# Channel stage: three images as one stationary operand on the way back, and the row sums of the two parities as products on their own rows of the array

## The chip, the core and the metric

The kernel runs on one NeuronCore of a Trainium2 chip. A core has a tensor engine (PE in the profile; PEld is its loading of stationary operands, which overlaps), a vector engine (DVE), a scalar engine (ACT), GpSimd (POOL), and queues that issue transfers (SP's above all). SBUF and PSUM have 128 partitions; PE reads SBUF and writes PSUM, which the kernel uses as eight banks of 512 fp32 numbers a partition. The metric is the device time of one execution in microseconds; all numbers here are fp32.

A product on PE has a stationary operand (K rows by M columns, loaded into the array) and a moving one (K rows by N columns). The result has M partitions and N numbers each. An fp32 product shows as two passes in the profile, each with its own load. Beside the whole array (128 by 128) a product may use half of its rows (64 by 128: K up to 64, at partition 0 or 64) or half of its columns (128 by 64: M up to 64).

## The reference

The input x has 32 images of 192 channels of 56 by 56 pixels. Four layers are applied, each as x = x + f(groupnorm(x)), with 32 groups of 6 channels: agent attention, a bidirectional linear recurrence (RWKV), a shift by whole pixels with a 3 by 3 Gaussian for every four channels, and a long convolution. The channel stage of the kernel computes the last two:

```python
# layer 2: every channel is shifted by the rounded offset and blurred with a 3x3 kernel of the rest
x = x + _L2_conv_ref(_gn(x), L2_conv_offset)
# layer 3: a 55x55 kernel k, made by a small network from positions, applied per channel over FFTs
xf = jnp.fft.rfft2(x, s); kf = jnp.fft.rfft2(k[0], s)
y = jnp.fft.irfft2(xf * kf[None], s)
x = x + y[..., Kh // 2:Kh // 2 + H, Kw // 2:Kw // 2 + W] + bias * _gn(x)
```

## The kernel before

The kernel first makes the spectra of the long filters (make_filter), then runs attention, then the recurrence (scan_pairs), which writes x to DRAM channel by channel, and then the channel stage (channel_blocks), which holds the 32 images of one channel at a time.

A channel's tile x has 114 partitions: 57 for the even images (56 pixel rows and one row of the group means) and 57 for the odd ones, the two "parities" s. Along a partition stand 16 pairs of images, 56 pixels each. The steps, with their lines:

- shift: the blur and shift are two products per quad of images (two pairs): L1589 with the quad as stationary operand and the row matrix moving, L1596 (DVE) scales into `turned`, L1607 with `turned` as stationary operand and the column matrix moving, L1615 adds to x, L1616 takes sums.
- centre: L1633 (DVE) subtracts the mean into `padded`, whose pixel rows are 64 apart, L1635 (ACT) squares, L1636 sums the squares. L1624 (PE) brings sums of the six channels of a group together, for the mean and for the variance.
- analyse: the row sums (`_rows_to_spectra`, L1757): a quad of `padded` is the stationary operand, 114 rows by 128 columns, and the cosines and sines `f1` move, 168 columns: 42 frequencies, cosine and sine, for each parity, with zeros for the other parity's rows. Three quads fill a PSUM tile; L1763 (ACT) copies it to `y` in four pieces. Then L1655 makes `re` and `im` in three batches of 5, 5 and 6 pairs, and six operations on DVE for each batch (L1662 to L1668) multiply with the filter's spectrum into `real` and `imag`, 84 partitions by 32 images of 42 numbers.
- synthesise, the way back: L1681 takes a pair of images (84 columns) of `real` or `imag` as stationary operand, 32 products a channel, four pairs to a PSUM tile, which L1688 (ACT) copies to `z`, 84 partitions (2 images of 42). L1698 multiplies `z` (moving, eight pairs, 448 columns) with `f4` (stationary, 84 rows by 114 columns), so that the even image of a pair goes to partitions 0 to 56 and the odd one to 57 to 113; L1700 and L1701 (DVE) scale and add to x, and two transfers write the channel out.

The loop at the end of channel_blocks interleaves these: channels come in groups of six, and while group n is shifted (two channels in each of three slots) and centred (two in each of three slots), group n - 1 is analysed, a channel a slot, and the channel of the slot before is synthesised. The four generators are advanced in a fixed pattern of steps; the order in which the instructions finally stand in each engine's queue is set when the program is built, by the Tile framework's scheduler, which also assigns the PSUM banks. At run time each engine takes its queue in order. PSUM has four banks for the tiles named ps (shift, row sums, L1624, the way back), two for re and two for im.

make_filter uses the same `_rows_to_spectra` six times near the start, with two PSUM buffers.

## Time and profile before

| what | value |
|---|---|
| median of 3 runs | 12293.82 us (12292.39 to 12298.46) |
| the profiled execution | 12294.66 us, span of its instructions 12292.8 us |
| mean granted TensorE clock | 0.966 of full speed |
| busy, of the span | PE 92%, PEld 58%, DVE 88%, ACT 50%, POOL 18% |
| channel stage, from its first instruction to the end | 8372 to 12292.8 us |
| of it, 10000 to 11000 us | PE 988.2, PEld 764.3, DVE 866.4, ACT 355.4, POOL 83.7 us busy; clock 1.00 |
| DMA in the stage | 17% of its engines, 43 GB/s |

Times are from the start of the span. "busy" of PE is the union of its passes, whose ends are modelled; how far apart passes start says more. A group is shown as line, engine, operation, output<-inputs, shape (rows*columns of the stationary operand, then what moves), count, busy time, mean length and the idle time of the engine just before it with what ended that. In an order of time, a line gives start, length, engine and the merged instructions.

### The profile page before, as it was taken

Reading aid. Unit: us, or ns where it says so; the run is one execution under the profiler, and the core shown is the slowest. Engines: PE = TensorE matmul, PEld = TensorE weight load, DVE = VectorE, ACT = ScalarE, POOL = GpSimd, SP = SyncE. Lnnn points to the kernel's source line nnn. Section 1 sums busy time; section 2 is a strip of 40 time slices with the busy share of each in tenths; the row PEclk is TensorE's granted clock in tenths of the full one; section 3 lists DMA queues with packets and bytes.
Section 4 is the critical chain, followed back from the end, with each engine's and each line's share of the span. In section 5 each row is a group of like instructions: output and inputs, shape, how many; then the busy total and the mean of one; then the engine's idle time right before and its main releaser. Section 6 shows DMA issues by size and latency. Waiting matters only on the chain. (4 is left out here: it accounts for less than half of the span.)

```text
span 12292.8 us, 164375 instructions
## 1 busy us (share of the span) xinstructions
PE 11329.2 (92%) x62734; PEld 7107.7 (58%) x62734; DVE 10836.4 (88%) x15489; ACT 6205.0 (50%) x11808; POOL 2250.7 (18%) x2228
## 2 busy tenths in 40 slices
PE   7999999999999999788888888888999999999999
PEld 3555555655555555333333333336777777777777
DVE  6888888888888887999999999997888888888888
ACT  3555555555555554566666666663333333333333
POOL 0000000000000000655555555551000000000000
PEclk9999999999999999999999999999999999999999
DMA  2111111111111111244344433442111111111111
GB/s 69 40 42 46 52 41 40 40 40 40 40 40 40 42 50 44 75 103 100 95 97 103 101 94 97 103 101 65 44 41 45 41 44 42 44 42 44 42 43 29
DMA packets 930055, 719.69 MB, mean 59 GB/s; under 512 B 770325, under 2 KB 807236, under 8 KB 920124
## 3 DMA queue, kind: packets, MB, share of 16 engines
q1 hardware_dynamic: 919020, 683.39, 21.7%
q10 hardware_dynamic: 10240, 25.70, 0.8%
q8 instruction: 500, 8.19, 0.3%
q14 instruction: 295, 2.42, 0.1%
HBM read 403.47 MB, written 240.65 MB: 52 GB/s over the span
## 5 line engine op out<-in xcount | busy, mean ns | idle before, releaser
L572 DVE SCALAR_TENSOR_TENSOR o<-v_a,att_w,o 128x896 f32<-128x896 f32 (+1 forms) x1024 | 1053.8, 1029 | 418.6 <-ACT v_a L546 291.5
L1763 ACT COPY y<-ps 64x252 f32<-64x252 f32 (+1 forms) x2376 | 808.2, 340 | 1135.0 <-PE ps L1757 1104.8
L1681 PE MATMUL ps<-fixed,real 84*84 84x112 f32 x6144 | 1090.9, 259 | 0.0
L1681 PE MATMUL ps<-fixed,imag 84*84 84x112 f32 x6144 | 1089.5, 259 | 0.0
L1688 ACT COPY z<-ps 84x448 f32<-84x448 f32 x768 | 405.6, 528 | 1218.5 <-PE ps L1681 1217.0
L1086 POOL MEMSET f<- 128x1 f32 x96 | 8.9, 99 | 4726.3 <-DMA st_c<-st 4721.3
L1681 PEld LDWEIGHTS ps<-fixed,real 84*84 84x84 f32 x6144 | 784.0, 153 | 134.2 <-issue 95.8
L1681 PEld LDWEIGHTS ps<-fixed,imag 84*84 84x84 f32 x6144 | 763.8, 153 | 0.0
L1079 ACT ACTIVATE q<-q 128x784 f32<-128x784 f32 x384 | 328.2, 855 | 802.5 <-DVE q L1074 633.1
L834 PE MATMUL ps<-sq,fixed 128*128 128x392 f32 x512 | 297.3, 743 | 428.6 <-ACT sq L1157 428.6
L572 DVE SCALAR_TENSOR_TENSOR o<-v_c,att_w,o 128x448 f32<-128x448 f32 (+1 forms) x1024 | 635.0, 620 | 5.1
L585 PE MATMUL ps<-xs_a,gk_a 128*98 128x448 f32 (+1 forms) x1536 | 637.1, 495 | 0.0
L589 ACT ACTIVATE pr<-ps,low 98x896 f32<-98x896 f32 (+1 forms) x384 | 352.3, 918 | 559.9 <-DVE low L587 559.9
L586 PE MATMUL ps<-xs_c,gk_c 125*98 125x448 f32 (+1 forms) x1536 | 631.6, 492 | 0.0
L1547 POOL TENSOR_TENSOR mat<-tap,tap 114x114 f32<-114x114 f32 x96 | 40.8, 425 | 3166.1 <-PE ps L1607 2313.2
L677 PE MATMUL ps<-gq_a,xs_a 128*112 128x294 f32 x1792 | 602.8, 417 | 19.2 <-DVE pq L682 19.2
L1698 PE MATMUL ps<-z,fixed 84*114 84x448 f32 x1536 | 608.8, 539 | 0.0
L834 PE MATMUL ps<-x,weights 128*128 128x392 f32 x1536 | 577.4, 519 | 27.5 <-DVE bv L1108 14.2
L678 PE MATMUL ps<-gq_c,xs_c 125*112 125x294 f32 x1792 | 594.5, 412 | 0.0
L1655 PE MATMUL re<-y,fixed 128*84 128x420 f32 (+1 forms) x1152 | 532.3, 543 | 8.7 <-ACT y L1763 7.6
L1655 PE MATMUL im<-y,fixed 128*84 128x420 f32 (+1 forms) x1152 | 526.9, 538 | 0.0
L690 ACT ACTIVATE pq<-pq 112x1176 f32<-112x1176 f32 x224 | 265.3, 1184 | 498.9 <-DVE pq L682 376.0
(367 smaller groups left out, 29245.2 us busy)
## 6 DMA issues: line engine op xcount, KB each, us to landing
x<-x SPq DMA_DIRECT2D x576, 392.0 KB
x<-x SPq DMA_DIRECT2D x512, 196.0 KB
x<-x SPq DMA_DIRECT2D x192, 399.0 KB
out_x<-x SPq DMA_DIRECT2D x384, 196.0 KB
x<-in_x SPq DMA_DIRECT2D x32, 1568.0 KB
x<-x SPq DMA_DIRECT2D x32, 1568.0 KB
x<-in_x SPq DMA_DIRECT2D x64, 392.0 KB
rd<-rd ACTq DMA_DIRECT2D x128, 196.0 KB
```

The source lines that it names most:

```text
L572: nc.vector.scalar_tensor_tensor(dst, tap(i), dww[:, t, i : i + 1], dst, ALU.mult, ALU.add)
L585: mm(ps[P2, h, :n], g[:, cols], xs_a[j][:, px], start=True, stop=False)
L586: mm(ps[P2, h, :n], gk_c[0:KC, 2 * j + h, cols], xs_c[j][0:KC, px], start=False, stop=True)
L589: nc.scalar.activation(pr[:, :, :n], ps[P2, :, :n], AF.Exp, bias=low[:, j, p : p + 1], accum_out=sums[:, j, p : p + 1])
L677: mm(ps[:SUB, i, :HA], xs_a[j][:, px], g, start=True, stop=False)
L678: mm(ps[:SUB, i, :HA], xs_c[j][0:KC, px], gq_c[0:KC, 2 * j + (q + i) // ns], start=False, stop=True)
L834: mm(out, aa, srcs[t][h], start=True, stop=False)
L1655: nc.tensor.matmul(ps[:, : n * 84], f2[:, i, :], y[:, i0 : i0 + n].rearrange("p g s u -> p (g s u)"), start=True, stop=True)
L1681: nc.tensor.matmul(ps[:84, i * 2 * S : (i + 1) * 2 * S], part[:, i0 + i].rearrange("p s u -> p (s u)"), f3[:, m, :], start=(m == 0), stop= ...
L1688: nc.scalar.copy(z[:, i0 : i0 + n].rearrange("p g m w -> p (g m w)"), ps[:84, : n * 2 * S])
L1698: nc.tensor.matmul(got, f4[:, m, :], z[:, i0 : i0 + n, m, :], start=(m == 0), stop=(m == 1))
L1763: nc.scalar.copy(y[64 * m : 64 * m + 64, 2 * g0 + i : 2 * (g0 + n) : 2], got[64 * i : 64 * i + 64, :, :, m, :])
```

## The change

Even and odd images now stand at partitions 0 to 56 and 64 to 120 of x, `padded` and the constants (PR, the number of partitions in use, goes from 114 to 121), with zeros between.

- Row sums: each quad gives two products instead of one, rows 0 to 56 and rows 64 to 120, each on its half of the array's rows, with only 84 columns moving. Four quads make a batch, with one PSUM tile for each parity, and each tile is copied to `y` in four pieces of 168 elements: 16 copies a channel in place of 12.
- Way back: the stationary operand of L1681 is three images (126 columns) instead of two, so 11 in place of 16 (the last one has two images), and `z` has 126 partitions.
- Last product: three images to a column of `z` no longer match even and odd. For nine (then seven) pairs of images there is a product for the pairs whose images 0 and 1 stand in one column, one for the pairs with images 1 and 2, and for the pairs that lie across two columns two products on half of the array's columns each. `f4` holds a stationary operand for each.
- Shift: the stationary operand of L1607 has 121 columns; `turned` is 64 apart; the x tiles are fifteen fixed ones, cleared once (partitions 32 to 63), as are the two `turned` tiles, and a channel is loaded by two transfers.

```diff
-    (114, (2 * 2 * NF,)), (128, (2, 2 * NF)), (84, (2, 2 * S)), (84, (2, 114)), (114, (114,)), (114, (114,)),
...
+PR = 64 + S + 1
...
+    (PR, (2 * NF,)), (128, (2, 2 * NF)), (84, (2, 2 * S)), (126, (2, 2 * PR + 128)), (PR, (PR,)), (PR, (PR,)),
...
-    f4 = np.zeros((2, NF, 2, 2, R))
-    for s in range(2):
-        f4[s, :, 0, s, :S], f4[s, :, 1, s, :S] = weight * cos, -weight * sin
+    f4 = np.zeros((3, NF, 2, 2 * PR + 128))
+    for i, c in ((0, 0), (1, 64), (1, PR), (2, PR + 64), (2, 2 * PR), (0, 2 * PR + 64)):
+        f4[i, :, 0, c : c + S], f4[i, :, 1, c : c + S] = weight * cos, -weight * sin
...
+    shifted = [cp.tile([PR, NI, S], F32, name=f"x{i}", tag=f"x{i}") for i in range(15)]
+    for t in shifted:
+        nc.vector.memset(t[32:64], 0.0)
+    sides = [cp.tile([2 * S, NG, 2, 64], F32, name=f"turned{i}", tag=f"turned{i}") for i in range(2)]
+    for t in sides:
+        nc.vector.memset(t[:, :, :, S + 1 : 64], 0.0)
+
...
 
         c = q.n * GROUP + j
         rows, cols = matrices(c // 4)
-        x = xp.tile([PR, NI, S], F32, name="x", tag="x")
-        nc.sync.dma_start(out=x, in_=x2[c].rearrange("s h g w -> (s h) g w"))
+        x, turned, W = shifted[c % len(shifted)], sides[c % 2], 2 * (S + 1)
+        for s in range(2):
+            nc.sync.dma_start(out=x[64 * s : 64 * s + S + 1], in_=x2[c, s])
         flat = x.rearrange("p g w -> p (g w)")
-        turned = wp.tile([2 * S, NG, 2, S + 1], F32, name="turned", tag="turned")
         for g0 in range(0, NG, 4):
             n = min(4, NG - g0)
             ps = psum()
             for g in range(n):
                 nc.tensor.matmul(
-                    ps[: 2 * S, g * PR : (g + 1) * PR],
+                    ps[: 2 * S, g * W : (g + 1) * W],
                     flat[:, (g0 + g) * 2 * S : (g0 + g + 1) * 2 * S],
                     rows,
                     start=True,
                     stop=True,
                 )
             nc.vector.tensor_tensor(
-                turned[:, g0 : g0 + n].rearrange("p g s h -> p (g s) h"),
-                ps[: 2 * S, : n * PR].rearrange("p (g h) -> p g h", h=S + 1),
+                turned[:, g0 : g0 + n].rearrange("p g s h -> p (g s) h")[:, :, 0 : S + 1],
+                ps[: 2 * S, : n * W].rearrange("p (g h) -> p g h", h=S + 1),
                 _bc(q.scale[:, j, g0 : g0 + n].rearrange("p g s -> p (g s)"), [2 * S, 2 * n, S + 1]),
                 ALU.mult,
             )
...
-                    turned[:, g0 + g].rearrange("p s h -> p (s h)"),
+                    turned[:, g0 + g].rearrange("p s h -> p (s h)")[:, 0:PR],
...
     def synthesise(q, j, product):
 
         c = q.n * GROUP + j
-        real, imag = product
-        z = wp.tile([84, NI, 2, S], F32, name="z", tag="z")
-        for i0 in range(0, NI, 4):
-            n = min(4, NI - i0)
+        parts = [t.rearrange("p g s u -> p (g s u)") for t in product]
+        z = wp.tile([126, NT, 2, S], F32, name="z", tag="z")
+        for i0 in range(0, NT, 4):
+            n = min(4, NT - i0)
             ps = psum()
+            rows = []
             for i in range(n):
-                for m, part in enumerate((real, imag)):
+                at = 126 * (i0 + i)
+                r = min(126, NB * 42 - at)
+                rows.append(r)
+                for m, part in enumerate(parts):
                     nc.tensor.matmul(
-                        ps[:84, i * 2 * S : (i + 1) * 2 * S],
-                        part[:, i0 + i].rearrange("p s u -> p (s u)"),
-                        f3[:, m, :],
-                        start=(m == 0),
-                        stop=(m == 1),
+                        ps[:r, i * 2 * S : (i + 1) * 2 * S], part[:, at : at + r], f3[:, m, :], start=(m == 0), stop=(m == 1)
                     )
-            nc.scalar.copy(
-                z[:, i0 : i0 + n].rearrange("p g m w -> p (g m w)"), ps[:84, : n * 2 * S]
-            )
+            full = rows.count(126)
+            for r, i, k in ((126, 0, full), (rows[-1], full, n)):
+                if i < k:
+                    nc.scalar.copy(
+                        z[:r, i0 + i : i0 + k].rearrange("p g m w -> p (g m w)"), ps[:r, i * 2 * S : k * 2 * S]
+                    )
             yield
         x = q.x[j]
-        for i0 in range(0, NI, 8):
-            n = min(8, NI - i0)
+        for p0 in range(0, NI, 9):
+            n = min(9, NI - p0)
+            k0, k = 2 * (p0 // 3), n // 3
             ps = psum()
-            got = ps[:PR, : n * S].rearrange("p (g w) -> p g w", w=S)
-            for m in range(2):
-                nc.tensor.matmul(got, f4[:, m, :], z[:, i0 : i0 + n, m, :], start=(m == 0), stop=(m == 1))
-            o = wp.tile([PR, 8, S], F32, name="o", tag="o")[:, :n]
-            nc.vector.tensor_tensor(o, got, _bc(q.rs[:, i0 : i0 + n], [PR, n, S]), ALU.mult)
-            nc.vector.tensor_tensor(x[:, i0 : i0 + n], x[:, i0 : i0 + n], o, ALU.add)
+            got = ps[:, : n * S].rearrange("p (g w) -> p g w", w=S)
+
+            sums = []
+            ev, od = z[:, k0 : k0 + 2 * k : 2], z[:, k0 + 1 : k0 + 2 * k : 2]
+            if k > 0:
+                sums += [
+                    ((got[:PR, 0 : 3 * k : 3], f4[:, :, 0:PR], ev),),
+                    ((got[:PR, 2 : 3 * k : 3], f4[:, :, PR : 2 * PR], od),),
+                    (
+                        (got[0:64, 1 : 3 * k : 3], f4[:, :, 2 * PR : 2 * PR + 64], ev),
+                        (got[64:128, 1 : 3 * k : 3], f4[:, :, 2 * PR + 64 : 2 * PR + 128], od),
+                    ),
+                ]
+
+            left, at = n - 3 * k, k0 + 2 * k
+            if left > 0:
+                r = min(126, NB * 42 - 126 * at)
+                sums.append(((got[:PR, 3 * k : 3 * k + 1], f4[:r, :, 0:PR], z[:r, at : at + 1]),))
+            if left == 2:
+                r = NB * 42 - 126 * (at + 1)
+                sums.append(
+                    (
+                        (got[0:64, 3 * k + 1 : 3 * k + 2], f4[:, :, 2 * PR : 2 * PR + 64], z[:, at : at + 1]),
+                        (got[64:128, 3 * k + 1 : 3 * k + 2], f4[:r, :, 2 * PR + 64 : 2 * PR + 128], z[:r, at + 1 : at + 2]),
+                    )
+                )
+            for beside in sums:
+                for m in range(2):
+                    for to, w, src in beside:
+                        nc.tensor.matmul(to, w[:, m], src[:, :, m], start=(m == 0), stop=(m == 1))
+            got = got[:PR]
+            o = wp.tile([PR, 9, S], F32, name="o", tag="o")[:, :n]
+            nc.vector.tensor_tensor(o, got, _bc(q.rs[:, p0 : p0 + n], [PR, n, S]), ALU.mult)
+            nc.vector.tensor_tensor(x[:, p0 : p0 + n], x[:, p0 : p0 + n], o, ALU.add)
             yield
         for s in range(2):
             nc.sync.dma_start(
-                out=out[s::2, c].rearrange("b h w -> h b w"), in_=x[(S + 1) * s : (S + 1) * s + S]
+                out=out[s::2, c].rearrange("b h w -> h b w"), in_=x[64 * s : 64 * s + S]
             )
 
     def centres(q, j):
...
 def _rows_to_spectra(nc, psum, padded, f1, y, ng):
 
 
+
     flat = padded.rearrange("p g w -> p (g w)")
-    for g0 in range(0, ng, 3):
-        n = min(3, ng - g0)
-        ps = psum()
+    for g0 in range(0, ng, 4):
+        n = min(4, ng - g0)
+        ps = [psum() for _ in range(2)]
         for g in range(n):
-            nc.tensor.matmul(
-                ps[:, g * 168 : (g + 1) * 168], flat[:, (g0 + g) * 128 : (g0 + g + 1) * 128], f1, start=True, stop=True
-            )
-        got = ps[:, : n * 168].rearrange("p (g s m u) -> p g s m u", s=2, m=2, u=42)
-        for i in range(2):
-            for m in range(2):
-                nc.scalar.copy(
-                    y[64 * m : 64 * m + 64, 2 * g0 + i : 2 * (g0 + n) : 2], got[64 * i : 64 * i + 64, :, :, m, :]
+            for s in range(2):
+                r = slice(64 * s, 64 * s + S + 1)
+                nc.tensor.matmul(
+                    ps[s][:, g * 84 : (g + 1) * 84], flat[r, (g0 + g) * 128 : (g0 + g + 1) * 128], f1[r], start=True, stop=True
                 )
+        for s in range(2):
+            got = ps[s][:, : n * 84].rearrange("p (g m u) -> p g m u", m=2, u=42)
+            for i in range(2):
+                for m in range(2):
+                    nc.scalar.copy(
+                        y[64 * m : 64 * m + 64, 2 * g0 + i : 2 * (g0 + n) : 2, s], got[64 * i : 64 * i + 64, :, m, :]
+                    )
 
 
 @with_exitstack
```

## The prediction

> **What bounds the kernel now.** I read the page first (engines, then the 40 slices), then the busy time of the last third slot by slot, then its groups with shapes kept apart, and last the order of time inside one slot.

> ```profile
> PE 11329.2 (92%) x62734; PEld 7107.7 (58%) x62734; DVE 10836.4 (88%) x15489; ACT 6205.0 (50%) x11808; POOL 2250.7 (18%) x2228
> ...
> PE   7999999999999999788888888888999999999999
> ```

> The change lies in the channel stage: slices 28 to 40, from 8372 us (its first instruction) to the end, where PE shows 9 throughout. I call a slot the stretch from one channel's row sums (first L1757) to the next one's. Six make a group: three in which two channels each are also shifted (L1589, L1607), three in which channels are centred. The next fence has the last shift slot of a group and its three centre slots; columns are length, then busy time of PE, PEld, DVE, ACT, POOL.

> ```profile
> 10043.79:10067.01 23.22, 22.94 (x167) 18.40 (x166) 19.08 (x34) 6.19 (x16) 3.21 (x6) 1.00 0.16 37
> 10067.01:10084.59 17.58, 17.37 (x114) 12.89 (x112) 16.06 (x28) 8.00 (x18) 0.00 (x0) 1.00 0.18 47
> 10084.59:10100.97 16.38, 16.17 (x102) 11.69 (x100) 14.63 (x25) 8.10 (x18) 0.00 (x0) 1.00 0.20 51
> 10100.97:10117.50 16.53, 16.21 (x101) 11.72 (x100) 16.08 (x27) 8.09 (x18) 0.00 (x0) 1.00 0.20 50
> ```

> PE waits 0.2 to 0.3 us a slot: its instruction stream is the slot. DVE is within 0.5 us of it in the last centre slot, ACT is half idle. So a microsecond on PE is a microsecond of the end, either way, 192 times. The groups from 9000 to 12000 us (count | busy, mean ns | idle before):

> ```profile
> L1681 PE MATMUL ps<-fixed,real 84*84 84x112 f32 x4756 | 844.4, 259 | 0.0
> ...
> L1763 ACT COPY y<-ps 64x252 f32<-64x252 f32 x1184 | 430.3, 363 | 828.0 <-PE ps L1757 814.1
> ...
> L1763 ACT COPY y<-ps 64x168 f32<-64x168 f32 x592 | 173.8, 294 | 8.7
> ```

> A product is two passes here (counts are double the program's). What a pass costs is the distance between successive starts in the timeline: 0.096 us for L1681 (112 moving columns), 0.142 for L1757 (168), 0.376 for L1698 (448), 0.100 for L1607 (114 stationary, 112 moving columns). L1624 (114 stationary, only 16 moving) also takes 0.100, and L468 (128 stationary, one moving) 0.112: there the load of the stationary operand sets the pace. ACT's copies follow each other at 0.377 (252 elements) and 0.305 us (168).

> ```profile
> 10084.59 2.44 PE L1757 MATMUL ps<-fixed,padded 114*128 114x168 f32 x16
> 10087.24 0.94 PE L1655 MATMUL re<-y,fixed 128*84 128x420 f32 x2 [0.21 <-ACT y L1763]
> ...
> 10085.70 4.24 ACT L1763 COPY y<-ps 64x252 f32<-64x252 f32 x12 [4.23 <-PE ps L1757]
> ```

> The one place where PE waits for ACT: `re` of the first batch needs the four copies of the first three quads. 1.11 us from the first row sum to the first copy, 4 x 0.377, and 2.65 us in all.

> The scan stage has products on half the rows (64*128) and half the columns (128*64):

> ```profile
> 8283.89 1.59 PE L837 MATMUL ps<-sq,fixed 64*128 64x392 f32 x8
> 8285.40 1.58 PE L844 MATMUL ps<-x,weights 128*128 128x392 f32 x4
> 8286.92 1.54 PE L847 MATMUL ps<-x,weights 128*64 128x392 f32 x8
> 8288.39 1.91 PE L834 MATMUL ps<-y,wogs 128*128 128x392 f32 x5
> ```

> Eight passes of L847 take 1.47 us, four times the 0.329 of one, plus 0.15: pairs run beside each other. So do those of L837 (1.51), both loads starting 7 ns apart. But each change of shape costs: the last pass before it stretches by 0.094, and the first load behind it is bare (0.05 for 64 columns, 0.10 for 128).

> **The change, part by part, per slot.**

> *Three images per stationary operand (L1681).* 64 passes at 0.096 = 6.14 us become 40 with 126 stationary columns and 4 with 84. Between the rows of 114 (0.100) and 128 columns (0.112), 126 gives 0.111: 40 x 0.111 + 4 x 0.096 = 4.81. **-1.33** (ends: load hidden, 0.096, -1.92; 0.112, -1.28). I take the line through both load-bound rows, since L1607 with the same 112 moving columns sits on it.

> [...]

> *Last product (L1698).* 8 passes at 0.376 = 3.01. Now nine pairs of images, then seven: first 8 full passes of 168 columns (0.142) and 4 pairs of half-column passes (0.142), 1.71; then 8 passes of 112 with 121 stationary columns (load-bound, 0.106), 4 pairs (0.096) and 4 passes of 56 (0.106), 1.65. Five shape changes come with it: into and out of the half columns twice, and on into the row sums: 0.15 + 0.17 + 0.15 + 0.20 + 0.09 = 0.76. Sum 4.12, **+1.10** (ends: changes free, +0.35; pairs not beside each other, +2.0).

> *Row sums on half the rows (L1757, L1763).* Before, three batches of six passes, four copies each. Now two batches, each two tiles (even, odd rows), eight copies of 168 elements. `re` of the first batch needs pairs 0 to 4, hence all eight copies: 8 x 0.112 (128 stationary columns, two beside each other) + 0.28 to the first copy, 8 x 0.305, 0.08 to `re`: 3.70 us against 2.65. In the built program the second batch isn't interleaved: four products of the even half, then four of the odd, whose tile takes the PSUM bank of the first tile and waits for ACT. They run one after the other (2 x 0.90) and end at 3.38, inside that wait. Queued behind `re` on PE: `im`, then all of the way back; behind those DVE's products. So **+1.05** where `re` follows the row sums (two centre slots), about **+0.9** where L1589, L1550 or L1624 comes first and must follow the odd half (2.59, 2.9, 3.85 us before). In a group's first slot both tiles of the second batch take the banks of the first, ACT's order has a square (0.95) after three of the copies, and the last L1624 and one row sum stand behind the odd half: walked through, `re` starts at 7.0 after the first L1624 instead of 3.85: **+3.1** (it could be +1 if the square is not late). Per group 3.1 + 3 x 0.9 + 2 x 1.05 = 7.9. For a lower end: without any wait for ACT the row sums would take 0.92 + 1.8 + 0.2 = 2.9, +0.25 a slot.

> [...]

> *Smaller.* L1607 with 121 stationary columns 16 x 0.006 = +0.10, L1624 +0.02. L1589 keeps 112. ACT: 16 copies for 12 (4.88 for 4.24), z copies 1.7 for 2.1: covered by its idle half, but for the eight on the path. DVE has the same elements. x arrives in two transfers for one: SP issues it many channels ahead (15 buffers) and covers it; uncovered, 1.0 us a channel (six issues took 6.07 at the stage's start). The way back has three steps for four, so the first half of L1698 moves ahead of the second shift; the z copies that it needs are then over 2 us old, and cover it; if not, one copy, 0.53.

> *Start of the stage.* DVE now clears 15 x 896 elements ahead of its first step on the offsets:

> ```profile
> 8371.82 0.06 DVE L1496 MEMSET eps<- 114x1 f32 x1 [11.69 <-SPq L1789]
> 8374.77 0.21 DVE L1501 TENSOR_SCALAR off<-off 114x96 f32<-114x96 f32 x1 [2.89 <-DMA off<-in_L_conv_offset]
> ...
> L906 DVE MEMSET wogs<- 128x128 f32 x1 | 0.2, 165 | 0.1
> ```

> 165 ns for 128 elements and 59 for one give 0.8 us each, 12 in all, 2.9 of it under the wait for `off`; POOL's taps and PE's first product hang on this: +9 (ends 3 and 12). The larger constants load under it. The filter at the start uses the same row sums with two PSUM buffers; its six blocks go from 9.67 to about 10.5 us: +5.

> **Sum.** Group: 7.9 + 6 x (1.10 - 1.33 + 0.12) = 7.2; times 32 = +231; with 9 and 5, +245. The profiled execution took 12294.66 (span 12292.8), 0.01% from the median 12293.82: 12294.7 + 245 = **12540 us**.

> **Rivals.**
> 1. *The wait for ACT does not form* (the copies go under other PE work). Then +0.25 a slot for row sums, (0.25 - 0.11) x 192 + 14 = +41: 12336. Against it: the program's order puts `re` straight behind, and the 0.21 us wait is there already.
> 2. *Faster.* Place: the first eight copies. If they went at 0.18 instead of 0.305 us, `re` would start at 2.7 and, with the first slot's +3.1 gone too, the slot would fall by 0.06; it decides there. [...] For it: ACT is half idle. Against: the 64x168 row has this very shape, and the second batch is not interleaved.
> 3. *DVE or ACT becomes the bound of centre slots.* ACT's square now stands behind the first z copy, about 2 us later, and DVE's L1636 waits for it; DVE's 15.7 us of work plus up to 2.5 of idle is 18.2 against PE's 17.4: +0.8 x 96 = +77: 12617. Against: the slot before had such idle (1.75) and PE did not notice.
> 4. *The two half-row loads go one after the other.* Then the first batch takes 1.8, +0.9 a slot: 12710. Against: the 7 ns of L837.

> **How the numbers follow.** Mine 0.70 (12440 to 12630, from the switch and first-slot terms), rival 1 0.08, 2 0.06, 3 0.11, 4 0.05. The range leaves out rival 2, most of 1, and 4: 12380 to 12660. 0.2% is 25 us, about what a measurement here can tell from no change. Slower by more: mine, 3, 4 and most of 1, 0.90; within 0.04; faster 0.06.

> **What would show it.** In the after trace: way-back passes 0.111 us apart; half-column pairs beside each other with 0.09 before and 0.05 behind; `re` about 3.7 us after the first row sum, with a wait on ACT's y copies of some tenths, the odd half waiting for ACT too; centre slots near 17.3, shift slots near 24. I am wrong if `re` starts within 2.8 us, if PE shows idle behind DVE, or if a shape change costs nothing.

## The result, and the profile after

The changed kernel takes 13097.67 us (median of 4 runs, 13094.46 to 13113.09) where the kernel before takes 12293.31 (4 runs beside it, 12292.39 to 12298.46): 1.0655 times as long, 95% interval 1.0638 to 1.0672. That is 804 us more; the prediction said 12540, 245 us more, with a range up to 12660. The profiled execution took 13096.12 us, its span 13094.3, at a mean granted TensorE clock of 0.914, where the kernel before had 0.966.

The page of the changed kernel, engines and slices:

```profile
PE 12040.0 (92%) x67438; PEld 7813.6 (60%) x67438; DVE 10855.8 (83%) x15506; ACT 6205.2 (47%) x12600; POOL 2231.6 (17%) x2228
...
PE   7999999999999997888888888799999999999999
...
PEclk9999999999999998999999999888888888888888
```

PE is busy in the channel stage (from slice 27 on) as it was, with a 9 in each. The line to read is PEclk: it shows 8 in the stage, where the kernel before has 9 in every slice:

```profile
PEclk9999999999999999999999999999999999999999
```

Busy time says nothing of it, because a product at half the clock is busy for about twice as long (1.69 us in place of 0.87 for the first two passes of `re` in the order of time below).

Now the slots of one group, as before from one channel's row sums (now L1804) to the next one's; columns are length, busy time of PE, PEld, DVE, ACT, POOL, then the granted clock, the share of DMA and GB/s:

```profile
10218.01:10243.30 25.29, 24.88 (x191) 20.56 (x191) 19.20 (x34) 6.26 (x20) 4.57 (x8) 0.93 0.13 33
10243.30:10267.04 23.74, 23.24 (x189) 19.59 (x188) 18.89 (x33) 6.26 (x20) 2.41 (x5) 1.00 0.16 38
10267.04:10286.91 19.87, 19.41 (x138) 15.23 (x137) 15.30 (x26) 8.05 (x22) 1.05 (x1) 0.91 0.16 42
10286.91:10310.43 23.52, 23.06 (x125) 17.82 (x124) 15.19 (x26) 7.89 (x22) 0.00 (x0) 0.71 0.13 34
10310.43:10334.95 24.52, 24.11 (x135) 18.70 (x135) 16.54 (x27) 7.27 (x22) 0.00 (x0) 0.72 0.13 34
10334.95:10365.34 30.39, 28.20 (x194) 22.58 (x193) 20.80 (x36) 7.49 (x23) 3.06 (x5) 0.83 0.13 33
13028.43:13045.37 16.94, 16.48 (x126) 12.92 (x125) 12.07 (x23) 6.26 (x20) 0.00 (x0) 1.00 0.13 25
```

Length goes with the clock. The second slot, at 1.00, takes 23.74 us; the prediction said "shift slots near 24". The last line is a slot near the end, with neither shift nor centring, at 1.00: 16.94 us, against 16.38 for such a slot before:

```profile
12211.50:12227.88 16.38, 16.17 (x101) 11.69 (x100) 11.98 (x23) 6.19 (x16) 0.00 (x0) 1.00 0.13 26
```

The slots at 0.71 and 0.72 take 23.5 and 24.5 where the prediction had 17.3 for a centre slot. PE's idle time in the slot from 10310.43 is 24.52 - 24.11 = 0.41 us: no wait explains seven microseconds.

The order of time on PE in two of these slots, the second and the fifth:

```profile
10243.30 2.01 PE L1804 MATMUL ps<-fixed,padded 57*128 57x84 f32 x24
10245.78 1.12 PE L1804 MATMUL ps<-fixed,padded 57*128 57x84 f32 x8 [0.46 <-ACT y L1811]
...
10249.59 0.87 PE L1667 MATMUL re<-y,fixed 128*84 128x420 f32 x2
...
10252.05 0.38 PE L1697 MATMUL ps<-fixed,imag 84*126 84x112 f32 x2
10252.27 0.38 PE L1697 MATMUL ps<-fixed,real 84*126 84x112 f32 x2
...
10310.43 2.01 PE L1804 MATMUL ps<-fixed,padded 57*128 57x84 f32 x24
10312.86 1.56 PE L1804 MATMUL ps<-fixed,padded 57*128 57x84 f32 x8 [0.41 <-ACT y L1811]
10314.34 1.69 PE L1667 MATMUL re<-y,fixed 128*84 128x420 f32 x2
...
10317.63 0.63 PE L1697 MATMUL ps<-fixed,imag 84*126 84x112 f32 x2
10318.05 0.64 PE L1697 MATMUL ps<-fixed,real 84*126 84x112 f32 x2
```

Both begin alike: 24 half-row passes in 2.01 us, a wait of some 0.4 us for ACT's copies, the last 8 half-row passes. In the second group of lines the last eight take 1.56 instead of 1.12, the same `re` 1.69 instead of 0.87, and products of the way back follow each other at 0.42 to 0.43 us where the first slot has 0.22. These passes run at about half speed, and 14 us later (from 10326.83) at full speed again: the clock records show 0.5 from 10313.37 to 10327.02. The clock fell during the row sums, and what pays for it is mostly the work behind them.

The clock records of the trace add up to 1360 us at half clock in the channel stage, counted from about its first row sums on (19 us in the kernel before). Half of that, 680 us, is an estimate of the time lost to it, good as long as PE is the bound; 124 us of the 804 are left for everything that the prediction worked out.

### The profile page after: what moved, and what is told of

Read it like the earlier page. It is cut to its first block, busy times and chain, and to the rows that moved or that the text cites. A ratio compares the mean times of both kernels' runs of the same rounds, so it can differ in the third digit from the quotient of the medians.

```text
span 13094.3 us, 174896 instructions
## 1 busy us (share of the span) xinstructions
PE 12040.0 (92%) x67438; PEld 7813.6 (60%) x67438; DVE 10855.8 (83%) x15506; ACT 6205.2 (47%) x12600; POOL 2231.6 (17%) x2228
## 5 line engine op out<-in xcount | busy, mean ns | idle before, releaser
L1811 ACT COPY y<-ps 64x168 f32<-64x168 f32 x3168 | 930.6, 294 | 1500.5 <-PE ps L1804 1459.7
L1703 ACT COPY z<-ps 126x448 f32<-126x448 f32 (+2 forms) x768 | 298.9, 415 | 1660.7 <-PE ps L1697 1660.7
L1697 PE MATMUL ps<-fixed,real 84*126 84x112 f32 (+1 forms) x4224 | 911.6, 302 | 0.0
L1697 PE MATMUL ps<-fixed,imag 84*126 84x112 f32 (+1 forms) x4224 | 907.6, 301 | 0.0
L1697 PEld LDWEIGHTS ps<-fixed,real 84*126 84x126 f32 (+1 forms) x4224 | 771.6, 220 | 165.3 <-issue 103.4
L1804 PE MATMUL ps<-fixed,padded 57*128 57x84 f32 x6144 | 711.7, 306 | 137.3 <-ACT y L1811 137.3
L1741 PE MATMUL ps<-z,fixed 126*121 126x168 f32 (+4 forms) x6912 | 792.8, 290 | 0.0
L1741 PEld LDWEIGHTS ps<-z,fixed 126*121 126x121 f32 (+2 forms) x6912 | 674.5, 163 | 174.9 <-issue 105.6
L1804 PEld LDWEIGHTS ps<-fixed,padded 57*128 57x128 f32 x6144 | 635.8, 211 | 178.8 <-ACT y L1811 166.8
L1697 PEld LDWEIGHTS ps<-fixed,imag 84*126 84x126 f32 (+1 forms) x4224 | 731.5, 216 | 2.7 <-issue 2.7
```

Source lines behind the costliest of these rows:

```text
L1697: nc.tensor.matmul(ps[:r, i * 2 * S : (i + 1) * 2 * S], part[:, at : at + r], f3[:, m, :], start=(m == 0), stop=(m == 1))
L1741: nc.tensor.matmul(to, w[:, m], src[:, :, m], start=(m == 0), stop=(m == 1))
L1804: nc.tensor.matmul(ps[s][:, g * 84 : (g + 1) * 84], flat[r, (g0 + g) * 128 : (g0 + g + 1) * 128], f1[r], start=True, stop=True)
L1811: nc.scalar.copy(y[64 * m : 64 * m + 64, 2 * g0 + i : 2 * (g0 + n) : 2, s], got[64 * i : 64 * i + 64, :, m, :])
```

## What to tell apart

- Theory A: half-row products, with a wait behind them, do too little in a window, and the clock halves; that is most of the loss.
- Rival B: the switches of shape on the way back do it.
- Rival C: the clock hardly matters, waits and switches cost the time.

A second question came up on the way: what the new way back is worth by itself.

## The experiments

All times are medians in us, ratios are against the kernel before on the same chip. "Half clock" is the time at half clock in the channel stage by the clock records; "wait" is PE's time waiting for ACT's `y` copies from 9000 to 12000 us, as far as the waits answer lists it (it leaves out the shortest). Both come from the profiled execution, which in e2, e5 and e6 took 10, 25 and 18 us less than the median.

| kernel | time | ratio (95%) | half clock | wait |
|---|---|---|---|---|
| before | 12293 | | 19 | 17 |
| changed | 13098 | 1.0655 (1.0638 to 1.0672) | 1360 | 90 |
| e1 full rows, new way back | 12363 | 1.0055 (1.0038 to 1.0072) | 30 | 56 |
| e2 half rows, old way back | 12766 | 1.0385 (1.0368 to 1.0403) | 503 | 59 |
| e3 changed, with fill | 12733 | 1.0356 (1.0338 to 1.0373) | 270 | 0 |
| e4 before, copies split | 12342 | 1.0036 (1.0023 to 1.0049) | 17 | 36 |
| e5 e1 in four steps | 12396 | 1.0080 (1.0064 to 1.0097) | 95 | 86 |
| e6 changed, half the copies | 12623 | 1.0264 (1.0247 to 1.0281) | 619 | 26 |
| e7 changed, all rows | 12700 | 1.0327 (1.0309 to 1.0344) | 272 | 69 |
| e8 before, copies twice | 12715 | 1.0338 (1.0320 to 1.0355) | 264 | 134 |
| e9 e1, sums on POOL | 12278 | 0.9990 (0.9981 to 1.0000) | 12 | 32 |
| e11 e9, clears on ACT | 12275 | 0.9987 (0.9978 to 0.9996) | 18 | 37 |
| e12 changed, whole columns | 12599 | 1.0246 (1.0231 to 1.0262) | 340 | 52 |
| e13 e1, whole columns | 12294 | 1.0002 (0.9993 to 1.0011) | 13 | 24 |

### One part alone: e1 and e2

e1 takes the row sums back to the whole array:

```diff
-    for g0 in range(0, ng, 4):
+    for g0 in range(0, ng, 3):
...
-            for s in range(2):
-                r = slice(64 * s, 64 * s + S + 1)
-                nc.tensor.matmul(
-                    ps[s][:, g * 84 : (g + 1) * 84], flat[r, (g0 + g) * 128 : (g0 + g + 1) * 128], f1[r], start=True, stop=True
+            nc.tensor.matmul(
+                ps[:, g * 168 : (g + 1) * 168], flat[:, (g0 + g) * 128 : (g0 + g + 1) * 128], f1, start=True, stop=True
+            )
...
```

> The changed kernel with the row sums as before: 121 rows of the whole array, both parities in one product of 168 columns, three groups to a PSUM tile, 12 copies a channel. The way back with three images on one stationary operand stays. Theory A (TensorE's granted clock falls to half in the channel stage because the row sums on half the rows, with the wait for ACT behind them, leave it too little to do for some microseconds, and that is worth about 680 us of the 804 lost): the clock is 1.00 in the channel stage again, and a channel is 0.11 us cheaper than before on the way back (-1.33 + 1.10 + 0.12): about 12,282 us with the 9 us of the memsets. Rival B (the switches of shape in the last product on the way back cost the clock): the clock stays near 0.85, about 12,900 or more. Rival C (the clock has nothing to do with it; the added wait and the switches cost the time by themselves): the clock stays near 0.85 or does not matter, and the time lies in proportion to the part left, 12,400 to 12,600.

e2 takes the way back instead:

```diff
-        z = wp.tile([126, NT, 2, S], F32, name="z", tag="z")
+        z = wp.tile([84, NI, 2, S], F32, name="z", tag="z")
...
-        for p0 in range(0, NI, 9):
-            n = min(9, NI - p0)
+        for i0 in range(0, NI, 8):
+            n = min(8, NI - i0)
...
```

> The changed kernel with the way back as before (two images on one stationary operand, the last product in 8 passes of 448 columns), and the row sums on half the rows kept. Theory A (the row sums and the wait behind them halve the clock): clock near 0.85, 12,294 + 253 for the row sums + 14 + some 600 for the clock, 13,100 to 13,200 us. Rival B (the switches of shape on the way back halve the clock): clock 1.00, about 12,560. Rival C: 12,560 whatever the clock says.

Measured: e1 12363 with the clock at 1.00, so Rival B falls as it was put: the new way back, by itself, leaves the clock alone. e2 12766 with the clock at 0.94 in the stage, so half rows alone do cost the clock, but 503 us of it, not 1360: Theory A's 0.85 and its 13,100 to 13,200 us were too much for this part. Neither part gives the whole: e1 is 66 us over the kernel before, e2 469, both together 804. 12766 less half of 503 is 12514, near what was expected for the row sums at full clock (12,560). Rival C expected parts of the loss in proportion; e1, with nearly all of the half clock gone, is 735 us faster than the changed kernel. That e1 takes 81 us more than the 12,282 expected is a second finding, taken up below.

### More work for PE: e3

```diff
                 ps = pp.tile([84, BANK], F32, name=name, tag=name)
+                if i0 == 0:
+                    nc.tensor.matmul(ps[:, : n * 84], f2[:, i, :], fixed[:, : n * 84], start=True, stop=True)
                 nc.tensor.matmul(
```

> The changed kernel with one more product ahead of the first re and one ahead of the first im of each channel: 128 rows, 420 moving columns, from constants, overwritten by the product that follows. It adds 4 passes of 0.35 us, 1.4 us of TensorE time a channel, at the place where TensorE has little to do, and changes nothing else. Theory A: the busier array keeps its clock, so that more work makes the kernel faster: the clock near 1.00, and 12,540 + 190 times (1.4 less up to 0.4 of wait that it fills) = 12,730 to 12,810 us. If it is not enough to keep the clock everywhere, between that and 13,098. Rivals B and C: the clock stays at 0.85 and the time rises to about 13,300 to 13,500.

The kernel with 384 more products is 365 us faster than the changed one. The row sums of one slot in order of time (L1806 are the row sums, L1668 the fill; the real product, L1669, follows at 12055.75):

```profile
12051.90 2.01 PE L1806 MATMUL ps<-fixed,padded 57*128 57x84 f32 x24
12053.84 0.94 PE L1668 MATMUL re<-fixed 128*84 128x420 f32 x2
12054.70 1.12 PE L1806 MATMUL ps<-fixed,padded 57*128 57x84 f32 x8
```

The scheduler of the instructions put the first fill where the wait was, between the half-row passes, and the clock from 10000 to 11000 us is 0.97. Rivals B and C expected 13,300 to 13,500 here. This is the plainest evidence that the clock, and not the half-row passes' own length, cost most of the time. It also gives the rest of the sum a second estimate: 13098 less 680 is 12418; and 12733, less half of 270, less 192 times (1.40 of fill less 0.46 of wait), is 12418 too. And 270 us at half clock are left although PE waits for nothing that the answer lists: nearly all of them lie in the first slots of the groups, at a mean clock of 0.87.

### Wait or rows: e4, e6, e7, e8

e4 lengthens the wait and leaves the products alone:

```diff
-                nc.scalar.copy(
-                    y[64 * m : 64 * m + 64, 2 * g0 + i : 2 * (g0 + n) : 2], got[64 * i : 64 * i + 64, :, :, m, :]
-                )
+                for s in range(2):
+                    nc.scalar.copy(
+                        y[64 * m : 64 * m + 64, 2 * g0 + i : 2 * (g0 + n) : 2, s], got[64 * i : 64 * i + 64, :, s, m, :]
+                    )
```

> The kernel before with each of ACT's copies after the row sums cut in two, one for each parity: 24 copies a channel for 12, the first re behind 8 copies of 126 elements for 4 of 252. The row sums stay on 121 rows of the whole array, so this makes a longer wait for ACT without the passes on half the rows. Eight copies at about 0.27 us (0.305 for 168 elements, 0.377 for 252) are 2.2 us against 1.5: TensorE waits 0.65 to 0.85 us where it waited 0.2. Theory A with the activity of the array, not the bare wait, as what trips the clock: the clock stays 1.00, and 192 times 0.65 make about 12,420 us. If any wait of this length trips it: clock 0.85 to 0.9, 12,900 or more.

Measured 12342: PE waits 0.43 us for `re` where it waited 0.21, as long as in the changed kernel's slots, and the clock stays at 1.00. The copies are cheaper than I took them to be, so the cost is 0.23 us a slot and not 0.65. A wait of 0.43 us behind products on 114 rows left the clock here at 1.00:

```profile
12193.26 0.94 PE L1655 MATMUL re<-y,fixed 128*84 128x420 f32 x2 [0.43 <-ACT y L1764]
```

e8 makes the wait long:

```diff
-                nc.scalar.copy(
...
+                for _ in range(2):
+                    nc.scalar.copy(
...
```

> The kernel before with each of ACT's copies after the row sums made twice. The result is the same; the first re stands behind 8 copies of 0.377 us for 4, so TensorE waits about 1.7 us where it waited 0.2, four times what the changed kernel waits, with every product on 114 or 128 rows. If the activity of a window decides, 1.7 us of full rows in 3.4 us is 0.42 to 0.47, at the edge: clock 0.95 to 1.00 and 12,294 + 192 x 1.5 = about 12,580 us, up to 12,700. If a wait of more than some tenths trips the clock: 0.85 to 0.9, 13,000 or more.

Measured 12715, clock 0.97. The waits of PE from 9000 to 12000 us (in total, times, longest):

```profile
PE ps L1589 <- ACT y L1764: 81.6, 57, 1.9
PE re L1655 <- ACT y L1764: 48.1, 66, 1.9
```

So waits of up to 1.9 us behind products on all rows did cost some clock here, 264 us at half clock, as a sum over the window would have it (the estimate was 0.42 to 0.47, "at the edge"). 12715 less half of 264 is 12583: the 12,580 expected at full clock; the 12,700 given as the upper end is just passed.

e6 does the reverse: half-row products, hardly a wait.

```diff
-                for m in range(2):
-                    nc.scalar.copy(
-                        y[64 * m : 64 * m + 64, 2 * g0 + i : 2 * (g0 + n) : 2, s], got[64 * i : 64 * i + 64, :, m, :]
-                    )
+                nc.scalar.copy(y[:, 2 * g0 + i : 2 * (g0 + n) : 2, s], got[:, :, i, :])
```

> The changed kernel with four copies of 128 rows behind each batch of row sums for eight of 64 rows. They write all of y, but not each value to its place: the exchange of the row halves is left out, and the result with it. TensorE's products, their shapes and their order stay; the wait for ACT goes. This asks whether the low activity of the half-row products alone halves the clock. In the changed kernel's trace a window of 3.4 us that was followed by a halved clock had its moving columns, weighted by the share of the 128 rows in use, at 0.18 to 0.42 of the window; windows that kept the clock had 0.49 and more. Without the wait the row sums have 1.0 us of weighted columns in 2.7 us and busier work around them, some 0.47 in the window: at the edge. If the sum over a window is what counts: clock 0.95 to 1.00, and 12,350 to 12,600 us. If half-row products trip the clock whatever stands around them: clock 0.87 or less, 12,900 or more.

Measured 12623 and, in the stage, a clock of 0.92 to 0.94: between the two expectations, 619 us at half clock. The waits from 9000 to 12000 us, first of the changed kernel, then of e6:

```profile
PE ps L1804 <- ACT y L1811: 90.1, 122, 2.2
```

```profile
PE ps L1804 <- ACT y L1810: 26.0, 47, 0.7
```

With less than a third of the wait, less than half of the half-clock time is left, but far from none: with half rows the clock fell here with 26 us of waits in all, as it did in e3 with none that the answer lists. This run also speaks for rows, and against the time in which columns move. Its windows before a fall had 0.61 in moving columns, not weighted, in the median, and up to 0.80; weighted by rows they had 0.32, and 0.47 at most. Counting passes beside each other once, they had columns moving for up to 0.60 of the window and lost the clock, while windows of e8, all rows in use, kept it from 0.41 on. What these runs can't tell apart is the share of the rows and the share of the whole array, rows times stationary columns: weighted by that, windows before a fall had up to 0.34 in the changed kernel and windows that kept the clock 0.41 and more, 0.36 and more in the kernel before; over all kernels it was up to 0.37 before a fall and 0.25 and more where the clock held, not much worse a division.

e7 keeps the tiles, the order and the eight copies of the changed kernel and fills the rows:

```diff
-                r = slice(64 * s, 64 * s + S + 1)
                 nc.tensor.matmul(
-                    ps[s][:, g * 84 : (g + 1) * 84], flat[r, (g0 + g) * 128 : (g0 + g + 1) * 128], f1[r], start=True, stop=True
+                    ps[s][:, g * 84 : (g + 1) * 84],
+                    flat[:, (g0 + g) * 128 : (g0 + g + 1) * 128],
+                    f1[:, 84 * s : 84 * (s + 1)],
+                    start=True,
+                    stop=True,
                 )
...
```

> The changed kernel with its two tiles of row sums, their order and their eight copies a batch, but each product taken over all 121 rows, with zeros in the weights of the other parity: the same results from products that go one after the other and keep the array's rows busy. TensorE's row sums grow from 0.9 + 1.8 us to 32 passes of 0.112, 3.6 us. Theory A: the clock is 1.00 again, so that a channel with more work in it is faster: the first re stands behind 1.9 us of products and eight copies of 0.305, 4.4 us for the 2.65 of the kernel before; 192 times 1.75, less 0.36 on the way back, with the first and last slots of a group as in e1: 12,650 to 12,750 us. If the wait or the switches on the way back trip the clock by themselves: 0.85 to 0.9 and 13,100 or more.

Measured 12700, as expected. The row sums of one slot:

```profile
12141.19 2.87 PE L1803 MATMUL ps<-fixed,padded 121*128 121x84 f32 x24
12144.31 1.12 PE L1803 MATMUL ps<-fixed,padded 121*128 121x84 f32 x8 [0.25 <-ACT y L1814]
12145.55 0.94 PE L1667 MATMUL re<-y,fixed 128*84 128x420 f32 x2
```

The products that ran beside each other now run one after the other, 24 passes in 2.87 us for 2.01, and the kernel is 398 us faster. (Running one after the other also makes columns move for longer; that rows count rests on e6 and e8, not on this run alone.) The clock was not 1.00 as Theory A said but 0.97: PE still waits for ACT 1.9 us in the first slot of a group, which has some 7 of its 29 us at half clock; in all 272 us, about e8's.

Over all kernels of this study, from 8900 to 12200 us, the windows that kept the clock had 0.34 and more, weighted by rows, and those before a fall 0.47 at most, as in e6; between the two either happened (the ends move by a few hundredths with the window into which a pass on the edge is put).

### What the half columns add: e12

```diff
-                        (got[0:64, 1 : 3 * k : 3], f4[:, :, 2 * PR : 2 * PR + 64], ev),
-                        (got[64:128, 1 : 3 * k : 3], f4[:, :, 2 * PR + 64 : 2 * PR + 128], od),
+                        (got[:PR, 1 : 3 * k : 3], f4[:, :, 2 * PR : 3 * PR], ev),
+                        (got[:PR, 1 : 3 * k : 3], f4[:, :, 3 * PR : 4 * PR], od),
...
```

> The changed kernel with the images that lie in two sets of three (weights of half the columns, two products beside each other) taken by two whole-width products one after the other, with zeros in the weights. The row sums on half the rows stay. No product on the way back uses half the array any more, and TensorE gets about 0.5 us more work a channel (8 passes of 0.142 for 4 pairs, 8 of 0.106 for 4 pairs, less the changes of shape). The way back with full row sums kept the clock at 1.00, the half rows with the old way back had 503 us at half clock, both together 1360: the question is whether the half columns are what adds. If so: the half-clock time goes to about 500 us, 12,730 to 12,800 us, faster by 300 with more work. If the halves of columns have no part in it: 13,150 to 13,200.

Measured 12599, 499 us faster than the changed kernel, with 340 us at half clock: less than e2's 503, and better than expected. It does not single out the half columns, though. In its trace the row sums of a centred slot run without a wait:

```profile
12160.89 2.54 PE L1806 MATMUL ps<-fixed,padded 57*128 57x84 f32 x32
```

PE's waits for ACT fell from 90 to 52 us with them: the order that the instructions came out in changed along with the products. The changed kernel's own trace limits the part of the half columns: of its 125 windows before a fall from 8900 to 12200 us, every one has half-row passes of the row sums in it, and only 34 have a pass on half columns as well. How much of the difference between 503 and 1360 belongs to half columns next to the row sums and how much to the order stays open, but most of the falls came without them.

### The way back by itself: e1, e5, e9, e13, e11

In e1 an ordinary centred slot takes 16.0 us for 16.4, 0.36 less than before, yet the kernel is 66 us slower. The first slot of a group takes 26.3 in the mean (25.2 to 27.1) for 23.2, and the last centred slot before it 18.0 for 17.7. The expectations below take this last slot for 16.4 before, which is an ordinary one; the 16.53 among the prediction's slots ends at the L1624 products, which belong to it too:

```profile
10117.50 1.28 PE L1624 MATMUL ps<-sums,fixed 114*114 114x16 f32 x12
10118.64 2.53 PE L1757 MATMUL ps<-fixed,padded 114*128 114x168 f32 x16
```

From row sums to row sums it is 17.67, 10100.97 to 10118.64. So one slot of a group is slow in e1, its first; the last centred one only fails to gain. ACT's order of time in a last centred slot:

```profile
10013.88 0.73 ACT L1807 COPY y<-ps 64x252 f32<-64x252 f32 x2 [6.08 <-PE ps L1801]
10014.64 0.95 ACT L1647 ACTIVATE sq<-padded 121x896 f32<-121x896 f32 x1
10015.61 3.49 ACT L1807 COPY y<-ps 64x252 f32<-64x252 f32 x10
```

The square of the centring stands between the copies that PE waits for, and `re` waits 1.14 us for them. In the first slot, from 10030.74 to 10057.84, PE is idle for 3.0 us, where the slot from 10118.64 before has 0.2; the three longest waits:

```profile
10033.42 0.84 PE L1801 MATMUL ps<-fixed,padded 121*128 121x168 f32 x4 [0.72 <-ACT y L1807]
...
10037.98 0.94 PE L1667 MATMUL re<-y,fixed 128*84 128x420 f32 x2 [1.06 <-DVE a L1678]
...
10040.40 1.80 PE L1601 MATMUL ps<-mat,x 121*112 121x114 f32 x16 [0.79 <-issue]
```

e5 asked whether the number of steps in the written order sets this:

```diff
-        for i0 in range(0, NT, 4):
-            n = min(4, NT - i0)
+        for i0 in range(0, NT, 3):
+            n = min(3, NT - i0)
```

> The kernel of e1_full_rows (row sums as before, way back with three images) with its way back cut into four steps of three sets of images in place of three steps of four, so that the written order of steps deals the way back out as before. In e1 an ordinary channel lost 0.36 us (16.01 for 16.38) and still the kernel was slower, by 1.6 us in the last centred channel of a group and 3.3 in the first of the next, where ACT now takes the square of the centring in the middle of the copies that the first re waits for. Theory A' (those two slots are a matter of the order on ACT, which follows from the number of steps): they go back to 16.0 and 22.6, a group loses 6 times 0.36 = 2.2 us, and with 11 us at the start of the stage the time is about 12,240 us. Rival (they lie in the way back itself): the time stays at 12,363. The clock is 1.00 either way.

Measured 12396; the last centred slot takes 17.6 us, as before, the first one 26.2 (25.3 where the clock was 1.00), and an ordinary one 16.6. Theory A' falls: in e5 the square no longer stands between those copies, and the first slot is slow all the same, now with waits of the row sums (L1801) for ACT of up to 1.6 us. e9 relieves DVE, e13 slows PE (the way back of e12, the row sums of e1):

```diff
-            nc.vector.tensor_tensor(x[:, p0 : p0 + n], x[:, p0 : p0 + n], o, ALU.add)
+            nc.gpsimd.tensor_tensor(x[:, p0 : p0 + n], x[:, p0 : p0 + n], o, ALU.add)
```

> The kernel of e1_full_rows with the last sum of the way back (x + o, two instructions of 0.56 and 0.67 us a channel) on GpSimd in place of DVE. With four steps in place of three the two slow slots of a group stayed (17.64 and 26.1 us), so their cause is not the number of steps. Theory A'': TensorE's centred channels became shorter (16.0 us) than what DVE and ACT need for one, so DVE comes late to the centring, the square comes late to ACT and lands among the copies. With 1.2 us less on DVE: the last centred slot 16.0 to 16.3 for 17.98, the first slot of a group 22.6 to 23.5 for 26.2, in all 12,235 to 12,280 us, under the kernel before. Rival (DVE is not what is late, or GpSimd's sums slow DVE as much): 12,363 or more.

> The kernel of e1_full_rows with the way back of e12_whole_columns: three images on one stationary operand, nothing on half the array anywhere. TensorE has about 0.5 us more a channel than in e1, 0.14 more than before. By Theory A'' (in e1 TensorE outran DVE) this makes an ordinary channel 16.5 us for 16.0 but the last centred slot and the first of a group fall back to 16.5 and 23: 12,310 to 12,350 us, no slower than e1 with more work on TensorE. By the rival (a slower TensorE is slower everywhere): 12,363 + 96 = 12,460.

e9 takes 12278: the last centred slot 17.0, the first 24.2, an ordinary one still 16.0. e13 takes 12294, 69 us less than e1, with more work on PE: an ordinary slot 16.4, the last centred one 17.4, the first 24.2. Both ends of the balance move the time the way Theory A'' says, and a slower PE is not slower here. Both slots are about 1 us over the expectation. In the last one that is the expectation's own slip: the products that bring the group's sums together (L1636) stand at its end, ten passes in 1.04 us in e1, and stood there before. In the first slot 2.1 of the 3.1 us that e1 had lost are gone, with DVE relieved as with PE slowed, which speaks for DVE's lateness as the larger part of the cause. Of the 1.0 that is left, 0.7 is the wait of the last row sums for ACT's copies, which e1, e9 and e13 have alike (18.0 us in 25 times from 9000 to 12000 us in e9) and the kernel before does not have; why it is there with the new way back stays open. The gain in e9 lies within 0.2%.

e11 moves the clears at the start from DVE to ACT (the copies read a column of zeros):

```diff
-        nc.vector.memset(t[32:64], 0.0)
+        nc.scalar.copy(t[32:64].rearrange("p g w -> p (g w)"), zero[32:64].to_broadcast([32, NI * S]))
...
```

> The kernel of e9_pool_adds with the 15 clears at the start of the channel stage on ACT, which is idle there, in place of DVE, where they stand ahead of everything (14.3 us, 10.7 of them on the way to TensorE's first product). Theory: 10 us less than e9_pool_adds, 12,225 to 12,270. Rival (the loads of x, which wait for the clears, are what the first product waits for): no change against e9_pool_adds.

Measured 12275, 3 us less than e9 and no measurable difference. The clears still stand in the way, on another engine: a step of the same chain of offsets (L1525) runs on ACT, behind them.

```profile
8376.16 12.70 ACT L1510 COPY x<-zero 32x896 f32<-32x896 f32 x15 [13.21 <-POOL zero L1508]
8388.88 0.44 ACT L1525 ACTIVATE gs<-gs 121x288 f32<-121x288 f32 x1
```

e11 has the lowest median of all, 0.9987 of the kernel before (0.9978 to 0.9996): about 0.1%, too little to call a gain.

## Why the prediction was wrong

The sign was right and the mechanism of the row sums as well; the size was off by 558 us, and the step that failed is one that the prediction never set down as a step: its sum has no term for the clock, which is to put that term at nothing without a reason. It took every duration from stretches with a granted clock of 1.00 and used them unchanged for a stage with half-row products and waits in it. The page of the kernel before showed 9 in PEclk throughout; that went with how full its products kept the array (no window under 0.44), and the change takes just that away (0.18 to 0.42 in the windows before a fall). In its place the runs showed 1360 us at half clock, worth about 680 of the 804 us by the estimate above; e3 and e7, with more work on PE, got 365 and 398 us of the time back. None of the four rivals named the clock, and each was worked out at full clock too; nor did one of the three signs of being wrong come up (`re` within 2.8 us, PE idle behind DVE, a free change of shape).

Its own terms, read where the clock was 1.00:

- *Three images per stationary operand, -1.33.* 44 passes start 0.110 us apart (predicted 0.111) and take 3.51 + 1.25 = 4.76 us (from the start of the first to what follows, in the slot from 10243.30) for 6.14: -1.38. Right.
- *Last product, +1.10.* 10258.01 to 10259.98 and 10265.02 to 10267.04, 3.99 for 3.01: +0.98. Right to 0.12; if the passes took what was reckoned (3.36), the five changes of shape came to 0.63 for 0.76.
- *Row sums to `re`, 3.70 for 2.65.* From 13028.43 the product behind the row sums starts at 13031.95, 3.52 us, with a wait of 0.46 for ACT ahead of the odd half, as described. The first batch runs beside itself: sixteen passes in 1.12 us. So rival 1 (the wait does not form) and rival 4 (the halves go one after the other) fall, and so does rival 2.
- *An ordinary slot at full clock.* 16.94 for 16.38, +0.56: -0.36 for the way back (16.02 in e1) and +0.92 for the row sums (in e2, with the row sums alone, such a slot takes 17.35 at full clock, +0.97). Predicted +0.8 to 0.9; 192 times the difference is some 60 us.
- *Group's first slot, +3.1.* Not to be read directly in the changed kernel, where that slot is never at full clock; its mean of 30.0 us less half of its time at half clock is 25.0, +1.8, an estimate. With full rows and the new way back (e1) the slot is 3.1 us longer; with half rows and the old way back (e2) it is 26.9 us, by the same estimate 24.1, +1.0. So the term was put down to the wrong part: +3.1 comes with the new way back, and half rows alone show about the +0.9 of the other slots. Rival 3 (DVE or ACT as the bound) is alive in e1, by e9 and e13, though mostly in the first slot and not in the centre slots; in the changed kernel PE waits for nothing but ACT's `y` copies, as far as the answer lists it.
- *Start, +9, and filter, +5.* The stage's first product comes 10.7 us later after its start than before, with 15 clears 0.94 us apart; the stage itself starts 11.8 us later, and the row sums of the filter end 10.4 us later, at 160.8 for 150.4. Nearly right for the start, and 5 to 7 too little for the filter.

Terms at full clock: 192 x 0.56 + 11 + 12 = 131 us, against 124 left over from the clock. The prediction's 245 was nearly twice too high there; 12418 us would have been inside its range, though under the 12440 to 12630 that it gave to its own mechanism. That the two errors, too much for the first slot and nothing for the clock, pull in opposite ways is luck: the sum missed by less than the clock alone.

## What to carry to other kernels

In five of the six slots of the group above the changed kernel ran 3 to 14 us at half clock, and what went with it was what the array did in each window of 3.413 us, moving columns times the share of rows in use: in the runs here 0.47 at most before a fall, 0.34 and more where the clock held. So before a change that makes products smaller in rows, or puts a wait among them, add up this sum for both kernels, and not only how long PE is busy. The granted clock of the profile before did not by itself tell the clock after (1.00 in the stage before, 0.85 after). When an engine with slack gets its work in another order, look at what has slipped in between the instructions that the bound engine waits for. And when slots are compared, cut them at the same instruction in both kernels.

## What was not expected of the hardware

- The TensorE clock halved in a slot in which PE was idle for 0.41 of 24.52 us, and in e3 with no wait that the answer lists. What went with the falls was array rows in use over a window of 3.413 us: 0.18 to 0.42 of the window before a fall, 0.49 and more where it held (changed kernel). Column time alone did not divide them: with passes beside each other counted once, up to 0.60 of the window before a fall in e6, and 0.41 where e8 kept the clock. In e6 it fell with 26 us of waits from 9000 to 12000 us, against 90 in the changed kernel.
- Filling idle array time with products whose results are thrown away made a kernel faster: 384 products, 365 us less (e3).
- Products with twice the rows, one after the other, in place of pairs that ran beside each other: 398 us less (e7).
